# Rotated FFN of a Perceiver block on one NeuronCore: quantised integers turned by transposing DMA transfers, residual added by an accumulating DMA transfer

## The chip, the cores and the metric

The kernel runs on one NeuronCore of a Trainium2 chip. TensorE (PE) multiplies, VectorE (DVE), ScalarE (ACT) and GpSimd (POOL) work on rows of data, SyncE (SP) issues most of the transfers, and 16 DMA engines move the bytes. The metric is the device time of one execution in microseconds (us); lower is better.

## The reference

Three layers follow one another, each on a layer-normalised input and added to its residual: cross attention, a delta-rule attention with an MLP, and a Hadamard-rotated, quantised FFN. Only the last is touched. `x` has 128 x 32 = 4096 tokens of 512 features; the FFN is 2048 wide.

```python
def act_quant(x):
    scale = 127.0 / jnp.clip(jnp.max(jnp.abs(x), axis=-1, keepdims=True), EPS)
    return jnp.clip(jnp.round(x * scale), -128.0, 127.0) / scale

def h_bitlinear(x, w):
    xq = act_quant(fwht(x))      # fwht: normalised Hadamard transform of the last axis
    wq = weight_quant(w)         # -1, 0, 1 times one scale
    return jnp.einsum('bsh,oh->bso', xq, wq)

gate = h_bitlinear(h, w_gate)
up = h_bitlinear(h, w_up)
x = x + h_bitlinear(jax.nn.silu(gate) * up, w_down)    # h = layernorm(x)
```

## The kernel before

The function `hadamard_ffn` works on 32 tiles of 128 tokens. The weights lie in SBUF as bf16 integers (`wg`, `wu`, `wd`); two DRAM arrays come from the stage before: `x2`, the residual, and `z2`, the centred rows after the first butterflies of the first Hadamard transform.

One tile goes through these steps, by the lines of the kernel before:

- `load` (932): SP loads a `zt` tile of `z2` three tiles ahead, and an `xt` tile of `x2` for the residual.
- `turned` (969-970): TensorE transposes `zt` (through the helper at line 97), ScalarE copies it to `zT`. `rotated` (939): four products with the 128 x 128 Hadamard matrix finish the transform in PSUM.
- `integers` (976-981): VectorE takes the row maximum (976) and works out a scale (948, 950, 951); `rounded` multiplies and adds a magic number on ScalarE (956) and subtracts it on VectorE (960) or, where its last argument is true, on ScalarE (958). The result `q` is bf16, 128 x 512.
- `integers_turned` (986): TensorE transposes `q` in four blocks into PSUM, ScalarE copies them to `qT`.
- `middle` (996-1002): in four groups of 512 columns, TensorE multiplies by `wg` and by `wu`; ScalarE applies SiLU (1001), VectorE multiplies both (1002) into `m`, 128 x 2048 in fp32.
- `butterflies` (126, 127): eight VectorE additions and subtractions on halves of `m`.
- `middle_turned` (1008-1009) and `rotated` (939): sixteen fp32 transposes of `m`, four copies to `mT` on ScalarE, sixteen products with the Hadamard matrix into four PSUM banks.
- `last_integers` (1016-1026): four maxima (1016), their maximum (1020), the scale, and four roundings into `q2`; ScalarE subtracts the magic number for groups 0 and 2, VectorE for 1 and 3.
- `last_turned` (1032-1033): sixteen bf16 transposes of `q2` on TensorE in two PSUM tiles, two copies to `q2T` on ScalarE.
- `finish` (1039-1043): sixteen products with `wd`, scaling on ScalarE into `xo` (1041), the residual `xt` added on POOL (1042), and a store that POOL issues (1043).

The loop at the end (1055-1083) lays several tiles over one another: in turn `i` it works on the first integers of tile `i+1`, the middle of tile `i`, the rotation and last integers of tile `i-1` and the finish of tile `i-2`. A scheduler puts the instructions of each engine into a fixed order, and each engine then runs its own list in that order, waiting on semaphores where an operand or a buffer isn't ready. All PSUM tiles of this stage share one pool of eight banks (`ps`), so a product can have to wait until an earlier bank has been read. SP's transfers are issued in order; an SP instruction that waits holds all behind it.

Of the kernel before, what the change touches and what calls it, by code (L numbers as in the profile page):

```python
# [11 lines left out]
BF = mybir.dt.bfloat16  # L12
AF = mybir.ActivationFunctionType
ALU = mybir.AluOpType
# [4 lines left out]
P = 128  # L19
D = 512  # L20
DC = D // P
# [12 lines left out]
IF = 2048  # L34
IC = IF // P
# [83 lines left out]
def butterflies(nc, a, b):  # L119

    n = a.shape[1] // P
    step = 1
    while step < n:
        i = a.rearrange("p (a c d) -> p a c d", c=2, d=step * P)
        o = b.rearrange("p (a c d) -> p a c d", c=2, d=step * P)
        nc.vector.tensor_add(o[:, :, 0, :], i[:, :, 0, :], i[:, :, 1, :])  # L126
        nc.vector.tensor_sub(o[:, :, 1, :], i[:, :, 0, :], i[:, :, 1, :])  # L127
        a, b, step = b, a, 2 * step
    return a
# [255 lines left out]
NG = NT // SG  # L385
# [513 lines left out]
def hadamard_ffn(g: Ctx, x2, z2, mv2, had, ffn, out):  # L899


    tc, nc = g.tc, g.nc
    c1, c2 = 1.0 / math.sqrt(D), 1.0 / math.sqrt(IF)
    NG = IF // D
# [5 lines left out]
    with tc.tile_pool(name="d_w", **right) as wp, tc.tile_pool(name="d_w2", **right) as wp2, stack:  # L910
# [19 lines left out]
        def load(i, src, name):  # L930
            t = xp.tile([P, D], FP, name=name)
            nc.sync.dma_start(t, src[i * P : (i + 1) * P, :])
            return t

        def rotated(xT, c0):

            pr = ps.tile([P, D], FP, name="ps")
            for c in range(DC):
                nc.tensor.matmul(  # L939
                    pr[:, c * P : (c + 1) * P], xT[:, c0 + c, :], hd, start=True, stop=True  # L940
                )
            return pr

        def scales(mx, c):


            m = st.tile([P, 1], FP, name="m")
            nc.vector.tensor_scalar(m, mx, c, Q_EPS, ALU.mult, ALU.max)
            qs = st.tile([P, 1], FP, name="qs")
            nc.vector.reciprocal(qs, m)  # L950
            nc.vector.tensor_scalar(qs, qs, c, 127.0, ALU.mult, ALU.mult)  # L951
            return m, qs

        def rounded(q, pr, qs, scalar=False):
            t = wk.tile([P, D], FP, name="t")
            nc.scalar.activation(t, pr, AF.Identity, bias=magic, scale=qs)  # L956
            if scalar:
                nc.scalar.activation(q, t, AF.Identity, bias=minus)
            else:
                nc.vector.tensor_scalar(q, t, MAGIC, None, ALU.subtract)  # L960

        def statistics(ns):

            nc.scalar.activation(rstd[:, ns], mv2[:, ns, 1], AF.Sqrt, bias=g.ln_eps)
            nc.vector.reciprocal(rstd[:, ns], rstd[:, ns])
            nc.vector.tensor_scalar_mul(rstd[:, ns], rstd[:, ns], c1)

        def turned(i):
            zT = wk1.tile([P, DC, P], FP, name="zT")
            nc.scalar.copy(zT, g.transposed(ps, z.pop(i), g.ident))  # L970
            return zT

        def integers(i, pr):

            mx = st.tile([P, 1], FP, name="mx")
            nc.vector.tensor_reduce(mx, pr, AX.X, ALU.max, apply_absolute_value=True)
            m, qs = scales(mx, rstd[:, i : i + 1])
            q = wk1.tile([P, D], BF, name="q")
            rounded(q, pr, qs)
            f = st.tile([P, 2], FP, name="f")  # L980
            nc.vector.tensor_scalar_mul(f, both, m)
            return q, f

        def integers_turned(q, f):
            qT = wk1.tile([P, DC, P], BF, name="qT")
            nc.scalar.copy(qT, g.transposed(ps, q, g.identb, BF))
            return qT, f

        def middle(qT, f):

            m = mp.tile([P, IF], FP, name="m")
            for k in range(NG):
                ks = slice(k * D, (k + 1) * D)
                pg = ps.tile([P, D], FP, name="ps")
                for dc in range(DC):
                    nc.tensor.matmul(pg, qT[:, dc, :], wg[:, dc, ks], start=dc == 0, stop=dc == DC - 1)  # L996
                pu = ps.tile([P, D], FP, name="ps")
                for dc in range(DC):
                    nc.tensor.matmul(pu, qT[:, dc, :], wu[:, dc, ks], start=dc == 0, stop=dc == DC - 1)  # L999
                s = wk.tile([P, D], FP, name="s")  # L1000
                nc.scalar.activation(s, pg, AF.Silu, scale=f[:, 0:1])
                nc.vector.scalar_tensor_tensor(m[:, ks], pu, f[:, 1:2], s, ALU.mult, ALU.mult)  # L1002
                yield m

        def middle_turned(m):
            mT = mp.tile([P, IC, P], FP, name="mT")
            for k in range(NG):
                pt = g.transposed(ps, m[:, k * D : (k + 1) * D], g.ident)
                nc.scalar.copy(mT[:, k * DC : (k + 1) * DC, :], pt)
            return mT  # L1010

        def last_integers(pr):

            mx = st.tile([P, NG], FP, name="mx4")
            for k in range(NG):
                nc.vector.tensor_reduce(  # L1016
                    mx[:, k : k + 1], pr[k], AX.X, ALU.max, apply_absolute_value=True
                )
            mx1 = st.tile([P, 1], FP, name="mx")
            nc.vector.tensor_reduce(mx1, mx, AX.X, ALU.max)  # L1020
            mm, qs = scales(mx1, c2)
            q = mp1.tile([P, IF], BF, name="q2")
            for k in range(NG):
                rounded(q[:, k * D : (k + 1) * D], pr[k], qs, k % 2 == 0)
            f = st.tile([P, 1], FP, name="fd")
            nc.vector.tensor_mul(f, mm, sd)
            return q, f

        def last_turned(q):
            qT = mp1.tile([P, IC, P], BF, name="q2T")  # L1030
            for k in range(2):
                pt = g.transposed(ps, q[:, k * IF // 2 : (k + 1) * IF // 2], g.identb, BF)
                nc.scalar.copy(qT[:, k * IC // 2 : (k + 1) * IC // 2, :], pt)  # L1033
            return qT

        def finish(i, x, qT, f):
            pd = ps.tile([P, D], FP, name="ps")
            for c in range(IC):
                nc.tensor.matmul(pd, qT[:, c, :], wd[:, c, :], start=c == 0, stop=c == IC - 1)  # L1039
            xo = wk.tile([P, D], FP, name="xo")  # L1040
            nc.scalar.activation(xo, pd, AF.Copy, scale=f)  # L1041
            nc.gpsimd.tensor_add(xo, xo, x)  # L1042
            nc.gpsimd.dma_start(out[i * P : (i + 1) * P, :], xo)

        n = NT // P
# [1 line left out]
        rstd = wp.tile([P, n], FP, name="rstd")  # L1049
        z = {i: load(i, z2, "zt") for i in range(3)}  # L1050
        nc.sync.dma_start(wd.rearrange("p c n -> p (c n)"), ffn[2][0])
        x = {}
        statistics(slice(0, late))
        f, m, q = integers_turned(*integers(0, rotated(turned(0), 0))), {}, {}
        for i in range(n + 2):
            if i + 3 < n:
                z[i + 3] = load(i + 3, z2, "zt")
            if i + 1 < n:
                zT = turned(i + 1)
            if i < n:  # L1060
                x[i] = load(i, x2, "xt")
                steps = middle(*f)
                m[i] = next(steps)
            if i == n // 2:
                statistics(slice(late, n))
            if i + 1 < n:
                f = integers(i + 1, rotated(zT, 0))
            if i < n:
                for _ in steps:
                    pass  # L1070
            if 0 <= i - 1 < n:
                mT = middle_turned(m.pop(i - 1))
            if 0 <= i - 2:
                q2, fd = q.pop(i - 2)
                q2T = last_turned(q2)
            if 0 <= i - 1 < n:
                q[i - 1] = last_integers([rotated(mT, k * DC) for k in range(NG)])
            if i + 1 < n:
                f = integers_turned(*f)
            if 0 <= i - 2:  # L1080
                finish(i - 2, x.pop(i - 2), q2T, fd)
            if i < n:
                m[i] = butterflies(nc, m[i], mp.tile([P, IF], FP, name="mb"))

# [2 lines left out]
def perceiver_block(  # L1087
# [26 lines left out]
    with tc.tile_pool(name="s_l", bufs=1, side="right", reuse_waits="tile") as sp:  # L1114
# [9 lines left out]
        def beside_mlp(b):  # L1124
# [9 lines left out]
            x2, z2, mv2, beside_mlp,  # L1134
        )
    hadamard_ffn(g, x2, z2, mv2, had, list(zip(fq, scales)), out)


# [57 lines left out]
```

## Time and profile before

| what | value |
|---|---|
| median of 3 runs | 3079.94 us (3078.09 to 3083.41) |
| the profiled execution | 3080.81 us, its span 3079.0 us |
| rotated FFN in the span | about 2415 to 3079 us |
| busy in the whole span | PE 95%, DVE 67%, ACT 35%, POOL 23% |

The profile is of one execution. Its groups name a line, an engine, an operation and `out<-in` tiles, then the count, the busy time, the mean of one in ns, and the idle time ahead of it with what ended it. Lines 97, 126, 127, 939, 956 to 960 lie in helpers, so groups are told apart by tile names. PEld is the loading of weights into TensorE, beside the products.

### The profile page before, as it was taken

The numbers are of one execution on the slowest core, as the hardware profiler recorded it, in microseconds if no ns is written. First come the engines' busy times: TensorE is split into PE (matmuls) and PEld (weight loads), VectorE is DVE, ScalarE is ACT, GpSimd is POOL, SyncE is SP. The second block draws the span as 40 slices with busy tenths as digits, with TensorE's granted clock in tenths as the row PEclk, the third lists the DMA queues.
The fourth block names the chain that finished last, engine by engine and source line by source line (L and its number), as shares of the span: only waits on it lengthen the run. The fifth ranks groups of instructions, "written<-read, shape, count | busy, mean of one in ns | idle before, by whom it ended". The sixth has DMA issues, their size and how long they took to land.

```text
span 3079.0 us, 42048 instructions
## 1 busy us (share of the span) xinstructions
PE 2934.2 (95%) x15558; PEld 1683.7 (55%) x15558; DVE 2059.5 (67%) x3432; ACT 1090.1 (35%) x1812; POOL 706.0 (23%) x995
## 2 busy tenths in 40 slices
PE   8999999999999999599999999999999899999997
PEld 3444344443333333367676666667777566666664
DVE  2353434326699797378778787878422599999996
ACT  1111111215656666312221112111111366666665
POOL 1121212112686675321212111011000010000001
PEclk9999999999999999799999999999999999999998
DMA  9797989863554544641423323131411111111110
GB/s 332 265 311 269 307 306 310 274 213 98 166 148 131 173 129 132 198 126 59 128 74 106 97 66 112 48 101 50 139 42 42 55 42 42 42 42 35 39 31 21
DMA packets 258236, 408.09 MB, mean 133 GB/s; under 512 B 68336, under 2 KB 170864, under 8 KB 254576
## 3 DMA queue, kind: packets, MB, share of 16 engines
q1 hardware_dynamic: 223856, 305.21, 31.7%
q0 software_dynamic: 34176, 100.19, 9.5%
q8 instruction: 124, 2.03, 0.3%
q14 instruction: 80, 0.66, 0.1%
HBM read 288.36 MB, written 93.85 MB: 124 GB/s over the span
## 4 chain that ended last, share of the span: by engine, by line
PE 41%; DVE 17%; ACT 5%; issue 3%; DMA 2%; SPq 0%; POOL 0%; DVEq 0%; POOLq 0%; ACTq 0%
PE pm L834 9%; PE pm L823 9%; PE pm L826 9%; PE pp L520 5%; PE ps L797 3%; DVE mb L127 3%; ACT t L956 3%; DVE mb L126 2%; DVE mx L1016 2%; DVE m L126 2%; PE pg L455 2%; PE ps L764 2%; DVE m L1002 1%; DVE m L127 1%; DVE W L442 1%
## 5 line engine op out<-in xcount | busy, mean ns | idle before, releaser
L823 PE MATMUL pm<-hT,wg 128*128 128x256 f32 x1408 | 342.1, 386 | 0.7 <-ACT hT L812 0.7
L826 PE MATMUL pm<-hT,wu 128*128 128x256 f32 x1408 | 333.3, 379 | 0.0
L436 DVE TENSOR_TENSOR pr<-L,W 128x1984 f32<-128x1984 f32 (+30 forms) x248 | 312.1, 1258 | 24.6 <-DMA L<-ld 20.6
L442 DVE TENSOR_TENSOR W<-W,pr 128x1984 f32<-128x1984 f32 (+30 forms) x248 | 309.0, 1246 | 3.2
L834 PE MATMUL pm<-wd,mT 128*128 128x512 f32 x704 | 307.2, 592 | 0.0
L823 PEld LDWEIGHTS pm<-hT,wg 128*128 128x128 f32 x1408 | 262.2, 191 | 57.5 <-issue 16.2
L826 PEld LDWEIGHTS pm<-hT,wu 128*128 128x128 f32 x1408 | 267.2, 190 | 36.2
L834 PEld LDWEIGHTS pm<-wd,mT 128*128 128x128 f32 x704 | 132.6, 190 | 160.8 <-issue 160.7
L828 ACT ACTIVATE sg<-pm 128x256 f32<-128x256 f32 x176 | 67.4, 383 | 350.1 <-PE pm L823 340.1
L829 DVE TENSOR_TENSOR mT<-pm,sg 128x256 f32<-128x256 f32 x176 | 73.8, 419 | 164.1 <-PE pm L826 150.0
L1042 POOL TENSOR_TENSOR xo<-xo,xt 128x512 f32<-128x512 f32 x32 | 42.7, 1336 | 581.6 <-ACT xo L1041 581.6
L996 PE MATMUL ps<-wq,qT 128*128 128x512 bf16 x512 | 133.1, 383 | 28.9 <-DVE m L1002 17.3
L956 ACT ACTIVATE t<-ps,magic,qs 128x512 f32<-128x512 f32 x160 | 117.6, 777 | 96.5 <-DVE qs L951 96.4
L461 POOL TENSOR_TENSOR kk<-kk,cm 128x256 f32<-128x256 f32 x128 | 135.5, 1058 | 2.1
L999 PE MATMUL ps<-wq,qT 128*128 128x512 bf16 x512 | 132.4, 381 | 2.2 <-DVE m L1002 2.2
L458 POOL DMA_DIRECT2D ld<-kk x128 | 92.2, 720 | 147.4 <-ACT kk L457 140.4
L346 PE MATMUL ps<-hT,wq 128*128 128x512 f32 x256 | 118.6, 623 | 7.2 <-ACT hT L339 7.2
L939 PE MATMUL ps<-hd,mT 128*128 128x128 f32 x1024 | 121.5, 277 | 0.0
L455 PE MATMUL pg<-kqm,kq 128*32 128x512 f32 x896 | 118.8, 601 | 2.1 <-DMA kqm<-kq 1.5
L302 PE MATMUL ps<-wo,aoT 128*128 128x512 f32 x256 | 118.8, 608 | 1.5 <-ACT aoT L295 1.5
L520 PE MATMUL pp<-hT,wk 128*128 128x512 f32 x256 | 118.6, 604 | 0.3 <-DVE acc L527 0.3
L1039 PE MATMUL ps<-wq,q2T 128*128 128x512 bf16 x512 | 117.2, 383 | 0.9 <-ACT q2T L1033 0.9
(217 smaller groups left out, 5220.6 us busy)
## 6 DMA issues: line engine op xcount, KB each, us to landing
kall<-in_ctxT_dram SPq DMA_DIRECT2D x32, 2056.0 KB
cx<-in_ctx_dram SPq DMA_DIRECT2D x32, 2048.0 KB
x<-xo POOLq DMA_DIRECT2D x64, 256.0 KB, 3.4
xt<-x SPq DMA_DIRECT2D x64, 256.0 KB
ld<-kk POOLq DMA_DIRECT2D x128, 128.0 KB, 2.5
pd<-kk POOLq DMA_DIRECT2D x128, 128.0 KB, 2.3
L<-ld SPq DMA_DIRECT2D x8, 2048.0 KB
pe<-pd SPq DMA_DIRECT2D x256, 64.0 KB
```

The lines of the kernel that those rows point to most:

```text
L126: nc.vector.tensor_add(o[:, :, 0, :], i[:, :, 0, :], i[:, :, 1, :])
L436: nc.vector.tensor_mul(pr[:, 0:n], bc(L[:, s, :, s + 1 : T].rearrange("p h t -> p t h"), HD), w[:, s].unsqueeze(1).to_broadcast([P, n, H4, ...
L442: nc.vector.tensor_sub(w[:, s + 1 :], w[:, s + 1 :], pr[:, 0:n])
L455: nc.tensor.matmul(pg[js], k[:, js], m[:, :, :, js], start=True, stop=True)
L461: nc.gpsimd.tensor_mul(kk[:, 1], kk[:, 1], cm.unsqueeze(1).to_broadcast([P, HH, T]))
L520: nc.tensor.matmul(pp.rearrange("p b t -> p (b t)"), w[n][:, dc, ec * P : (ec + 1) * P], hT[:, dc, :], start=dc == 0, stop=dc == DC - 1,)
L823: nc.tensor.matmul(pg, wg[:, dc, fs], hT[:, dc, :], start=dc == 0, stop=dc == DC - 1)
L826: nc.tensor.matmul(pu, wu[:, dc, fs], hT[:, dc, :], start=dc == 0, stop=dc == DC - 1)
L834: nc.tensor.matmul(pd, mT[:, fc, i * P : (i + 1) * P], wd[:, fc, :], start=fc == 0, stop=fc == FC - 1,)
L956: nc.scalar.activation(t, pr, AF.Identity, bias=magic, scale=qs)
L996: nc.tensor.matmul(pg, qT[:, dc, :], wg[:, dc, ks], start=dc == 0, stop=dc == DC - 1)
L999: nc.tensor.matmul(pu, qT[:, dc, :], wu[:, dc, ks], start=dc == 0, stop=dc == DC - 1)
```

## The change

The first integers `q` and the last integers `q2` are transposed by one transfer each, from SBUF to SBUF, that SP issues, in place of TensorE transposes and ScalarE copies. All four roundings of `q2` end on ScalarE. The first transfer is issued directly after `q` is rounded, inside the turn; the finish moves one turn later (tile `i-3`, in the middle of the turn, so the loop has one more turn). The residual is no longer loaded into a tile and added on POOL: a transfer issued by POOL adds rows of `x2` to `xo` in SBUF, and SP then stores `xo`.

```diff
         def integers_turned(q, f):
             qT = wk1.tile([P, DC, P], BF, name="qT")
-            nc.scalar.copy(qT, g.transposed(ps, q, g.identb, BF))
+            nc.sync.dma_start_transpose(qT, q)
             return qT, f
...
             for k in range(NG):
-                rounded(q[:, k * D : (k + 1) * D], pr[k], qs, k % 2 == 0)
+                rounded(q[:, k * D : (k + 1) * D], pr[k], qs, True)
...
         def last_turned(q):
             qT = mp1.tile([P, IC, P], BF, name="q2T")
-            for k in range(2):
-                pt = g.transposed(ps, q[:, k * IF // 2 : (k + 1) * IF // 2], g.identb, BF)
-                nc.scalar.copy(qT[:, k * IC // 2 : (k + 1) * IC // 2, :], pt)
+            nc.sync.dma_start_transpose(qT, q)
             return qT
 
-        def finish(i, x, qT, f):
+        def finish(i, qT, f):
...
             nc.scalar.activation(xo, pd, AF.Copy, scale=f)
-            nc.gpsimd.tensor_add(xo, xo, x)
-            nc.gpsimd.dma_start(out[i * P : (i + 1) * P, :], xo)
+            nc.gpsimd.dma_start(xo, x2[i * P : (i + 1) * P, :], accum_op=ALU.add)
+            nc.sync.dma_start(out[i * P : (i + 1) * P, :], xo)
...
-        x = {}
         statistics(slice(0, late))
-        f, m, q = integers_turned(*integers(0, rotated(turned(0), 0))), {}, {}
-        for i in range(n + 2):
+        f, m, q, done = integers_turned(*integers(0, rotated(turned(0), 0))), {}, {}, {}
+        for i in range(n + 3):
...
             if i < n:
-                x[i] = load(i, x2, "xt")
                 steps = middle(*f)
...
             if i + 1 < n:
-                f = integers(i + 1, rotated(zT, 0))
+                f = integers_turned(*integers(i + 1, rotated(zT, 0)))
+            if 0 <= i - 3:
+                finish(i - 3, *done.pop(i - 3))
...
-            if 0 <= i - 2:
-                q2, fd = q.pop(i - 2)
-                q2T = last_turned(q2)
             if 0 <= i - 1 < n:
-                q[i - 1] = last_integers([rotated(mT, k * DC) for k in range(NG)])
-            if i + 1 < n:
-                f = integers_turned(*f)
-            if 0 <= i - 2:
-                finish(i - 2, x.pop(i - 2), q2T, fd)
+                q2, fd = last_integers([rotated(mT, k * DC) for k in range(NG)])
+                done[i - 1] = last_turned(q2), fd
```

In the changed kernel's own numbering the large transfer is line 1031, the products with `wd` 1037, `xo` 1039, the accumulating transfer 1040 and the store 1041; the lines up to 1027 keep their numbers.

## Prediction

> **What bounds the kernel now.** I read the profile from coarse to fine: the windows of the last stage, its groups of instructions, its waits, and the timeline of one token tile. The rotated FFN runs from about 2415 to 3079 us of the span. In its steady part the windows show (columns: busy us and instruction count of PE, PEld, DVE, ACT, POOL, then granted clock, DMA share, GB/s):
>
> ```profile
> 2550.00:2650.00 100.00, 94.62 (x647) 63.40 (x646) 91.89 (x149) 63.06 (x100) 9.30 (x11) 1.00 0.13 41
> 2650.00:2750.00 100.00, 94.63 (x646) 63.32 (x644) 91.88 (x148) 63.08 (x101) 9.15 (x10) 1.00 0.14 44
> ```
>
> Two engines are nearly full and the DMA engines are 13% busy. From 2550 to 2950 us line 1016 runs 80 times, four to a tile: 20 tiles in 400 us, **20.0 us a tile**. The groups of that window that the change touches:
>
> ```profile
> L127 DVE TENSOR_TENSOR mb<-m 128x1024 f32<-128x1024 f32 x41 | 72.2, 1761 | 0.0
> ...
> L1033 ACT COPY q2T<-ps 128x1024 bf16<-128x1024 bf16 x40 | 40.3, 1105 | 0.0
> ...
> L958 ACT ACTIVATE q<-t,minus 128x512 bf16<-128x512 f32 x41 | 29.6, 721 | 0.0
> L97 PE MATMUL ps<-identb,q 128*128 128x128 bf16 x400 | 28.9, 219 | 0.0
> L960 DVE TENSOR_SCALAR q<-t 128x512 bf16<-128x512 f32 x61 | 25.8, 423 | 27.2 <-ACT t L956 26.7
> ...
> L986 ACT COPY qT<-ps 128x512 bf16<-128x512 bf16 x20 | 11.7, 586 | 22.9 <-PE ps L97 22.9
> ```
>
> The waits say that ScalarE waits for the second scale, and TensorE for PSUM banks that late evictions hold:
>
> ```profile
> ACT t L956 <- DVE qs L951: 63.8, 21, 3.8
> ...
> PE ps L996 <- DVE m L1002: 13.8, 8, 1.7
> PE ps L996 <- ACT t L956: 8.3, 13, 0.7
> ```
>
> So besides the full engines there is a ring of dependences. The timeline shows one turn, from the end of one rotation (line 939 from mT, which ended at 2701.82) to the end of the next:
>
> ```profile
> 2706.36 1.32 POOL L1042 TENSOR_TENSOR xo<-xo,xt 128x512 f32<-128x512 f32 x1 [17.19 <-ACT xo L1041]
> ...
> 2706.53 2.23 DVE L127 TENSOR_TENSOR mb<-m 128x1024 f32<-128x1024 f32 x1
> ...
> 2709.95 0.14 DVE L951 TENSOR_SCALAR qs<-qs 128x1 f32<-128x1 f32 x1
> ...
> 2710.12 1.45 ACT L956 ACTIVATE t<-ps,magic,qs 128x512 f32<-128x512 f32 x2 [2.60 <-DVE qs L951]
> ...
> 2714.01 0.79 ACT L956 ACTIVATE t<-ps,magic,qs 128x512 f32<-128x512 f32 x1
> ...
> 2714.67 1.86 ACT L1001 ACTIVATE s<-ps,f 128x512 f32<-128x512 f32 x3
> ...
> 2716.38 2.09 ACT L1009 COPY mT<-ps 128x512 f32<-128x512 f32 x4
> ...
> 2717.39 3.79 PE L939 MATMUL ps<-hd,mT 128*128 128x128 f32 x32
> ```
>
> The segments are 8.3 (maxima and scale on VectorE), 3.9 (roundings), 3.4 (SiLU and first copy) and 3.8 us (rotation): 19.4; neighbouring turns take up to 20.6. One butterfly takes 2.23 us beside POOL's residual addition, the others 1.22.
>
> **What the Trainium skill says.** "SBUF — State Buffer", Who interferes with whom: a VectorE instruction with two SBUF inputs contends with a GpSimd instruction that reads SBUF. The trace agrees: 2.23 against 1.22 us. "DMA: Bandwidth & Descriptors", Latency and other measured facts: a DMA transpose reached 261 GB/s; no run here shows one. Same page, SDMA does more than copy: its unit is a 256-byte tile. "VectorE: DVE Perf Modes", The three transpose paths: one 128x128 bf16 block takes 390 ns on TensorE and 1309 ns by DMA.
>
> **The change, part by part, per tile.**
> TensorE loses 20 transposes of integers. In the timeline their two groups hold the queue 0.99 + 0.42 us. PE's issue sum is now 6.86 (lines 996, 999) + 3.42 (1039) + 3.65 + 0.95 (939) + 2.26 + 0.57 (97, fp32) + 1.41 = 19.1; it becomes 17.7. VectorE loses two roundings (2 x 0.43) and the stretch (1.0): 18.4 to 16.5. ScalarE loses 2 x 1.0 + 0.5 of copies and gains two of line 958 (0.61 each in sequence). Neither is the new bound; the ring is, so I add it up in the instruction order of the changed program.
>
> (a) End of rotation to scale. The four reductions of line 1016 now stand after one butterfly and follow the rotation's groups, the last ending about 0.8 after it; then four unstretched butterflies (4 x 1.2) and small operations: 6.0 with the hand-over instead of 8.3.
> (b) Roundings. ScalarE now runs four t (0.67 each), four q (0.61) and xo (0.58) before the next tile's t: 5.7 instead of 3.9.
> (c) That t, three SiLUs (0.57 each) and the first copy: 3.0 instead of 3.4, as the sixteen transposes no longer stand in between.
> (d) Rotation: 3.8.
> Sum 18.5 us, above PE's 17.7. Gain 1.5 us over some 30 steady tiles: **-45**.
>
> **The new path.** Measure from the first t. The second rounding ends at 5.1, the next tile's at 7.1. SP issues the large transpose (512 KB), then the small one (128 KB). The small one is wanted at 13.0, when TensorE begins the next tile. Lower price: 261 GB/s, that is 2.0 and 0.5 us. Upper working price: packets. The DMA view (packets, MB, share of 16 engines' time) of a window of small packets, 1300 to 1400 us, 870 bytes on average:
>
> ```profile
> q1 hardware_dynamic: 10415, 9.06, 31.8%
> ```
>
> and of this stage (2420 to 3079 us; the last figure is the median from issue to landing):
>
> ```profile
> q1 hardware_dynamic: 8127, 15.45, 8.4%
> ...
> out_dram<-xo POOLq DMA_DIRECT2D x32, 256.0 KB, 3.2
> ```
>
> 31.8% of 16 x 100 us over 10,415 is 49 ns each. The large transpose is 2,048 pieces of 256 bytes, 128 to an engine: 6.3 us; the small one 1.6. For issue and first byte I take 1.3 and for landing 0.8 us, an estimate inside the 3.2 us that the 256 KB store takes from issue to landing. By the low price the small one is issued at 7.3, behind nothing that matters, and lands at L = 7.3 + 1.3 + 0.5 + 0.8, about 10. By the high price it stands behind the large one: L = 5.3 + 1.3 + 6.3 + 1.6 + 0.8 = 15.3. From its landing to the end of that tile's rotation TensorE has 17.2 us of work (its 17.7 less the zt transposes), and 6.0 of (a) stands before t, so two periods are at least L + 23.2. At L = 10 or 13 the ring's 18.5 stands; at 15.3 the period is 19.3; at 16.8 it is today's 20.0. I take a price below 5 us for the large one, since DMA is idle otherwise: 18.5.
>
> The large transpose itself has a whole tile of slack: its product moved one tile later. The accumulating transfer replaces POOL's addition; SP's store waits for it, and behind that store stand the next zt load and the next tile's transposes, not due for 13 us. Priced from the 256 KB store's 3.2 up to the 6.3 us that such a store took in the crowded first 300 us, it is hidden: 13 us cover it, and only beyond them would it delay the transposes. POOL's own wait is only for xo.
>
> **Ends.** Filling: wd's 2 MB stand on SP's queue ahead of the first small transpose, and the first tiles have no other PE work to hide one: estimate +4 (0 to 8). Draining: after the last rotation, rounding on ScalarE alone costs +1.2, the transpose instead of PE and copies (2.5 us in the trace) +1.7, accumulate and then store, against a 1.25 addition and a store, +2.5: about +6 (4 to 10).
> Total -45 + 4 + 6 = -35. The profiled execution took 3080.81 (span 3079.0, 1.8 around it), 0.9 above the median of the runs: 3080 - 35 = **3045**. With a ring between 18.0 and 19.0 and both ends at their bounds, 3028 to 3065.
>
> **Rivals.**
> 1. Packets cost what the window says (49 ns). Period 19.3, gain 0.7 x 30 = 21, ends +11: about 3070. For it: the piece size; against it: the skill's measured rate is three times faster. It blends into no change where the period is 19.65 (L 16.1).
> 2. Slower: the two transposes on SP's one queue become the ring. The place is the wait of the next tile's first product (line 996) for qT; the point is where both together take over some 9 us (L above 16.1). Price: in this stage q1's 8,127 packets took 8.4% of 16 x 659 us, 109 ns each. At that, 14 + 3.5 us: L = 25. The first product then frees the first SiLU, which stands on ScalarE ahead of t, and the period is L + 1.7 = 26.7: 6.7 x 31 + 12 = +220, about 3300. If blocks went one after another at 1309 ns (21 + 5.2 us, L 33.7) it would be 35.4 a tile, 3570. For it: a larger transfer stands ahead of the urgent one, and nothing in this trace transposes by DMA. Against it: that rate would leave 16 engines nearly unused.
> 3. The ring stays at 19.6, because ScalarE's longer row of roundings (b) delays the PSUM banks that TensorE waits for: gain 12, ends +10, 3078. Against it: (a) gains more than (b) loses.
>
> **How the numbers follow.** Forecast 0.60 (3045, own range 3028 to 3065); rival 1 0.11; rival 3 0.06; rival 2 0.23. Range 3028 to 3110: it holds the forecast, rivals 1 and 3 and the mild end of rival 2. 0.2% is 6 us, about what a measurement here tells from no change. Faster: the forecast and 0.08 of rival 1, 0.68. Within 0.2%: the other 0.03 of rival 1 and 0.04 of rival 3, 0.07. Slower: rival 2 and 0.02 of rival 3, 0.25.
>
> **What would show it.** Right: some 18.5 us between groups of line 1016; no 2.2 us butterfly; qT landing before TensorE asks; ScalarE's wait for the scale shorter. Wrong: line 996 waiting for a DMA each tile, SP's queue held in the transposes, or ScalarE's t later than 6 us after the rotation.

## The result, and the profile after

The changed kernel takes 3045.19 us (median of 4 runs, 3042.59 to 3050.57), the kernel before, on the same chip, 3081.68 us (3078.09 to 3083.64). The ratio is 0.9885, 95% interval 0.9868 to 0.9902: 1.2% faster. The profiled execution took 3042.59 us, its span 3040.8.

The first product of the FFN for tile 0 and the last rotation of tile 31 divide the stage into three parts, read from the two timelines:

| part of the span, us | before | after | difference |
|---|---|---|---|
| earlier stages, which the change doesn't touch | 2415.0 | 2410.0 | -5.0 |
| filling: first transpose of `zt` to first product of line 996 | 8.0 | 12.0 | +4.0 |
| middle: from there to the end of the last rotation | 633.3 | 590.4 | -42.9 |
| draining: from there to the end | 22.8 | 28.4 | +5.6 |

The first row is no effect: in the traces of all the kernels below, whose earlier stages are the same, that part ends anywhere from 2403.8 to 2415.0 us. So the middle part, which starts inside the stage, is the better measure of a variant, and it is given below beside each median.

In the steady part (2550 to 2950 us) line 1016 runs 88 times, where it ran 80 times: 22 tiles in 400 us where there were 20. Such a count can be off by most of a tile; the ends of the rotations give 18.25 us a tile after 19.8 (alternating 19.3 and 20.6), and tile times below are taken from them. The windows of the changed kernel (columns as before):

```profile
2550.00:2650.00 100.00, 96.26 (x590) 63.40 (x600) 89.53 (x149) 63.16 (x106) 5.51 (x6) 1.00 0.42 82
2650.00:2750.00 100.00, 96.88 (x576) 61.39 (x586) 91.27 (x149) 61.64 (x103) 4.60 (x5) 1.00 0.38 78
```

TensorE does a tile in 18.2 us and is 97% busy, without the 1.4 us a tile of the transposes; DMA went from 13 to about 40%. The groups of the same 400 us:

```profile
L958 ACT ACTIVATE q<-t,minus 128x512 bf16<-128x512 f32 x88 | 58.5, 718 | 0.0
...
L127 DVE TENSOR_TENSOR mb<-m 128x1024 f32<-128x1024 f32 x44 | 53.5, 1216 | 0.0
```

The mean of that butterfly fell from 1761 to 1216 ns: the stretch beside GpSimd's addition is gone. Four ScalarE roundings a tile stand where two stood. The waits (us in total, times, longest):

```profile
ACT t L956 <- DVE qs L951: 75.7, 22, 3.7
...
PEld L996 <- DMA qT<-q: 5.1, 7, 1.1
```

ScalarE still waits for the second scale in every tile, 3.4 us on average (before, 63.8 us in 21 waits, 3.0). TensorE waits for the small transpose in a third of the tiles, by 0.7. One turn, from the end of a rotation to the end of the next:

```profile
2703.82 0.72 PE L939 MATMUL ps<-hd,mT 128*128 128x128 f32 x5
...
2710.04 0.15 DVE L951 TENSOR_SCALAR qs<-qs 128x1 f32<-128x1 f32 x1
...
2710.22 1.45 ACT L956 ACTIVATE t<-ps,magic,qs 128x512 f32<-128x512 f32 x2 [2.90 <-DVE qs L951]
2711.56 1.33 ACT L958 ACTIVATE q<-t,minus 128x512 bf16<-128x512 f32 x2
...
2715.90 0.79 ACT L956 ACTIVATE t<-ps,magic,qs 128x512 f32<-128x512 f32 x1
...
2718.95 3.84 PE L939 MATMUL ps<-hd,mT 128*128 128x128 f32 x32 [0.23 <-ACT mT L1009]
```

From 2704.54 to 2710.22 are 5.7 us (maxima and scale), to 2715.90 another 5.7 (roundings), to 2718.95 3.1 (SiLU and first copy), to 2722.79 3.8 (rotation): 18.25.

The start and the end pay. The first product of the stage, and the end of it:

```profile
2421.99 1.49 PE L996 MATMUL ps<-wq,qT 128*128 128x512 bf16 x3 [9.12 <-DMA qT<-q]
...
3017.91 1.33 ACT L958 ACTIVATE q<-t,minus 128x512 bf16<-128x512 f32 x2
...
3024.94 6.17 PE L1037 MATMUL ps<-wq,q2T 128*128 128x512 bf16 x16 [9.05 <-DMA q2T<-q]
...
3032.12 0.85 POOL L1040 DMA_DIRECT2D xo<-x  x1 [11.17 <-ACT xo L1039]
3036.14 0.33 SPq L1041 DMA_DIRECT2D out_dram<-xo  x1
```

With nothing else to run, TensorE waits for both transposes. The last rounding ends at 3019.24 and the product begins at 3024.94: by the 512 KB transpose 5.7 us pass, though not by it alone, since the accumulating transfer of the tile before is issued at 3020.11 and runs beside it (see the run pool_add). The last accumulating transfer holds the store back by 4.0 us.

### The profile page after: what moved, and what is told of

It reads as the page before. It is cut to its first block, busy times and chain, and to the rows that moved or that the text cites. A ratio compares the mean times of both kernels' runs of the same rounds, so it can differ in the third digit from the quotient of the medians.

```text
span 3040.8 us, 40815 instructions
## 1 busy us (share of the span) xinstructions
PE 2895.6 (95%) x14856; PEld 1647.0 (54%) x14918; DVE 2010.3 (66%) x3368; ACT 1052.8 (35%) x1780; POOL 664.0 (22%) x963
## 4 chain that ended last, share of the span: by engine, by line
PE 38%; issue 23%; DVE 4%; DMA 2%; POOL 1%; ACT 0%; SPq 0%; POOLq 0%; DVEq 0%; ACTq 0%
PE pm L823 8%; PE pm L826 8%; PE pm L834 8%; PE pp L520 5%; PE ps L797 4%; PE pg L455 2%; PE ps L764 2%; DVE W L442 1%; DVE pr L436 1%; DMA xs<-x 1%; POOL xo L1040 1%; DMA wd<-in_WdownT_dram 1%; PE ps L97 1%; PE pm L455 0%; PE pn L579 0%
## 5 line engine op out<-in xcount | busy, mean ns | idle before, releaser
L1040 POOL DMA_DIRECT2D xo<-x x32 | 29.1, 908 | 589.1 <-ACT xo L1039 589.1
L996 PE MATMUL ps<-wq,qT 128*128 128x512 bf16 x453 | 124.3, 381 | 17.1 <-DMA qT<-q 15.3
L999 PE MATMUL ps<-wq,qT 128*128 128x512 bf16 x511 | 132.2, 381 | 1.5
L939 PEld LDWEIGHTS ps<-hd,mT 128*128 128x128 f32 x1024 | 118.7, 194 | 16.4 <-ACT mT L1009 16.1
```

Of the source, the lines that this page charges most:

```text
L939: nc.tensor.matmul(pr[:, c * P : (c + 1) * P], xT[:, c0 + c, :], hd, start=True, stop=True)
```

## The experiments

The prediction's theory: a ring of dependences sets the tile, before and after; the change shortens it where a butterfly was stretched and by moving the reductions, and gives part back where all roundings are on ScalarE. The main rival: TensorE's work sets the tile, and the transposes taken from it are the gain. Where nothing else is said a variant is made from the kernel before, and the ratio is to that kernel, on the same chip.

**accum_alone.** Only the residual: no `xt` load, no addition on GpSimd.

```diff
-            nc.gpsimd.tensor_add(xo, xo, x)
-            nc.gpsimd.dma_start(out[i * P : (i + 1) * P, :], xo)
+            nc.gpsimd.dma_start(xo, x2[i * P : (i + 1) * P, :], accum_op=ALU.add)
+            nc.sync.dma_start(out[i * P : (i + 1) * P, :], xo)
```

> The kernel before with the accumulating transfer alone: POOL's residual addition and the residual's loads go, SP stores; all transposes stay on TensorE. Theory (the ring sets the tile): the 2.2 us butterfly falls to 1.2, so the tile takes about 19.0 to 19.2 us instead of 20.0, TensorE's own 19.1 being the next floor; over 31 tiles -28 us, and the drain adds 2.5: about 3056. Rival (the stretch was hidden behind TensorE): tile unchanged, drain only, about 3084.

3044.09 us, 0.9886 (0.9865 to 0.9907); middle part 602.7. This part alone gives all that the change gives. The butterflies are at 1.22 us; the window of this kernel:

```profile
2650.00:2750.00 100.00, 98.70 (x676) 66.75 (x675) 91.89 (x155) 65.29 (x104) 5.08 (x6) 1.00 0.17 43
```

TensorE is 98.7% busy at 18.8 us a tile: with the ring 1 us shorter, TensorE with all its transposes is practically full. The theory named the mechanism; its size was 12 us too small.

**small_alone.** Only the 128 KB transpose by transfer, issued directly after `q`.

```diff
-            nc.scalar.copy(qT, g.transposed(ps, q, g.identb, BF))
+            nc.sync.dma_start_transpose(qT, q)
...
-                f = integers(i + 1, rotated(zT, 0))
+                f = integers_turned(*integers(i + 1, rotated(zT, 0)))
```

> The kernel before with the small transpose (q to qT) alone by a transfer; everything else, POOL's addition too, as before. Theory (ring): TensorE's queue loses only 0.42 us that does not lie inside the ring's longest part, so at most 0.3 us a tile, against +3 us of filling: 3070 to 3083. Rival (TensorE's sum sets the tile): 0.42 x 31 = -13 and +3: 3072. Rival (the transfer comes late): line 996 waits for it each tile and the time is above 3090.

3073.37 us, 0.9982 (0.997 to 0.9993); middle part 626.9, 19.6 us a tile. The time lies in the range of the theory and next to the 3072 of the first rival, so this run doesn't tell the two apart; the late transfer, which would have been above 3090, is excluded. The stretch is still there:

```profile
L127 DVE TENSOR_TENSOR mb<-m 128x1024 f32<-128x1024 f32 x41 | 71.2, 1736 | 0.0
```

**large_alone.** Only the 512 KB transpose by transfer, with the finish one turn later as the change has it; GpSimd's addition and the shared rounding stay.

```diff
-            for k in range(2):
-                pt = g.transposed(ps, q[:, k * IF // 2 : (k + 1) * IF // 2], g.identb, BF)
-                nc.scalar.copy(qT[:, k * IC // 2 : (k + 1) * IC // 2, :], pt)
+            nc.sync.dma_start_transpose(qT, q)
...
+            if 0 <= i - 3:
+                finish(i - 3, x.pop(i - 3), *done.pop(i - 3))
...
-            if 0 <= i - 2:
-                finish(i - 2, x.pop(i - 2), q2T, fd)
```

> The kernel before with the large transpose (q2 to q2T) alone by a transfer, and the finish one turn later; small transposes on TensorE, POOL's addition kept, roundings shared as before. Theory (ring): the sixteen transposes leave the stretch between the copies and the rotation, and the finish's place moves POOL's addition away from the butterflies: 18.6 to 19.0 us a tile, -35, drain +3: about 3050. Rival (TensorE's sum): 19.1 less 0.99 = 18.1 plus the old 0.9 of waits, 19.0: -31 and +3, 3054. Rival (a late transfer): it has a whole tile of slack, so only a slower filling or draining would show, and nothing would be above 3082.

3032.34 us, 0.9841 (0.9811 to 0.9871); middle part 585.9. It beats the changed kernel by 13 us although it does less of the change: something that it leaves out must cost time. All butterflies take 1.22 us here too, so their stretch went without the addition being removed, as the expectation had it; only a small VectorE instruction (line 981) takes 0.65 us instead of 0.21. The next run tests what the move alone does.

**move_alone.** Only the order: the finish, and with it GpSimd's addition, one turn later; both transposes stay on TensorE.

```diff
-            if 0 <= i - 2:
-                q2, fd = q.pop(i - 2)
-                q2T = last_turned(q2)
+            if 0 <= i - 2 < n:
+                q2, fd = q.pop(i - 2)
+                done[i - 2] = last_turned(q2), fd
...
+            if 0 <= i - 3:
+                finish(i - 3, x.pop(i - 3), *done.pop(i - 3))
...
-            if 0 <= i - 2:
-                finish(i - 2, x.pop(i - 2), q2T, fd)
```

> The kernel before with only the order changed: finish (and with it GpSimd's addition) one turn later, where the changed kernel has it; both transposes stay on TensorE, the roundings stay shared, and the addition stays on GpSimd. If the stretched butterflies (2.23 us beside the addition) are what cost before, the addition now falls beside instructions that it doesn't stretch: all butterflies 1.22 us, the tile at TensorE's floor of 18.8 us as with the accumulating transfer alone, 31 x 1.2 = 37 less, some 3 back for a longer end: 3046 (3040 to 3052). If instead large_alone was fast because TensorE lost the 16 products of the transpose, the tile stays at 20.0 us and the time is 3075 to 3085.

3053.14 us, 0.9925 (0.99 to 0.9951); middle part 609.6. The timeline of this kernel around one addition, and its window:

```profile
2723.49 1.27 POOL L1042 TENSOR_TENSOR xo<-xo,xt 128x512 f32<-128x512 f32 x1 [16.82 <-ACT xo L1041]
```

```profile
2550.00:2650.00 100.00, 98.36 (x680) 66.06 (x679) 88.83 (x154) 67.39 (x109) 10.97 (x12) 1.00 0.13 40
```

The addition still takes 1.27 us and all butterflies take 1.22: what stretched one of them was that they met. With no instruction taken away, 24 us of the middle part go, and TensorE is again 98% busy. The time is 1 us above the range expected.

**large_twice.** The changed kernel, with each large transpose issued a second time, into a tile that nothing reads, ahead of the small one.

```diff
             nc.sync.dma_start_transpose(qT, q)
+            again = mp1.tile([P, IC, P], BF, name="q2X")
+            nc.sync.dma_start_transpose(again, q)
```

> The changed kernel with every large transpose issued twice, the second into a tile that nothing reads, ahead of the small one on SP's queue. Theory (price of the transposes as in the prediction's second rival): the large one's data takes about 3.5 us (5.7 from the last rounding to its first product in the drain, less 2.1), so the small one lands some 3.5 us later than today's 13.5 us after the first rounding, at 17; the period becomes L/2 + 11.6 = 20.1, +1.9 x 31 and +4 at the ends: about 3107. Rival (the transfers are hidden with room to spare): under +8, below 3053. Rival (much slower, the two queue up and the period is L + 1.7 with a second transpose of 6.3): above 3140.

3058.36 us, 0.9935 (0.9913 to 0.9957); middle part 608.1, 17.6 above the changed kernel, 18.9 us a tile. SP's queue and TensorE's waits in this kernel:

```profile
2702.91 1.86 SPq L1031 DMA_TRANSPOSE q2T<-q  x1
2704.82 5.45 SPq L1033 DMA_TRANSPOSE q2X<-q  x1
2710.37 1.22 SPq L986 DMA_TRANSPOSE qT<-q  x1
```

```profile
PEld L996 <- DMA qT<-q: 39.0, 21, 3.0
PE ps L996 <- DMA qT<-q: 26.4, 15, 2.5
```

Doubled, the transfer does become what TensorE waits for in every tile: the place of the prediction's rivals 1 and 2 is right, and so is the period of rival 1. From the first `t` to the product that takes `qT` the timeline has 15.2 us on average, and (15.2 + 23.2) / 2 = 19.2. The expectation missed by 49 us because it made the small transpose land some 3.5 us later; by the timelines its product begins only some 2 us later than in the changed kernel (13.1 on average). The small transpose is issued 12.2 us after the first `t`, where the changed kernel issues it after 7.2, but its product follows 3.0 us after the issue, where that one's takes about 6. So in the changed kernel part of these 6 us is not its own: it is issued while the large one's packets are still moving.

**half_finish.** The changed kernel with 8 of the 16 products of `finish`.

```diff
-            for c in range(IC):
-                nc.tensor.matmul(pd, qT[:, c, :], wd[:, c, :], start=c == 0, stop=c == IC - 1)
+            for c in range(IC // 2):
+                nc.tensor.matmul(pd, qT[:, c, :], wd[:, c, :], start=c == 0, stop=c == IC // 2 - 1)
```

> The changed kernel with 8 of finish's 16 products a tile: half of the down projection is left out, and the output lacks it. TensorE loses 8 x 0.21 = 1.7 us a tile and no wait of the ring changes. If the ring of maxima, roundings, SiLU and rotation sets the tile, as my prediction held, it stays at 18.2 us, TensorE's busy share falls from 97 to about 88%, and the time is 3043 within 4. If TensorE is what sets the tile after the change (96.9% busy), the tile falls until the next floor, VectorE's 16.4 us of work: to 16.5 to 17.0 us, 31 x 1.2 to 1.7 = 37 to 53 us less, about 2992 to 3008.

3040.88 us, 0.9887 (0.9862 to 0.9912); middle part 585.3, still 88 maxima in 400 us.

```profile
2550.00:2650.00 100.00, 89.56 (x541) 62.49 (x540) 86.40 (x145) 63.16 (x105) 4.23 (x5) 0.95 0.41 82
```

TensorE falls to 90%. The turns of this kernel aren't even: two in three take 17.7 us and one takes 19.3, because there the rotation takes 1.6 us longer:

```profile
2628.11 3.84 PE L939 MATMUL ps<-hd,mT 128*128 128x128 f32 x32 [0.97 <-ACT mT L1009]
2645.78 5.46 PE L939 MATMUL ps<-hd,mT 128*128 128x128 f32 x32 [0.97 <-ACT mT L1009]
```

From 2646.6 to 2650.0 the granted clock is one half, and so it is in each of the long turns. That their mean is again 18.2 is chance. In an undisturbed turn TensorE is busy for 15.9 of 17.7 us: it has lost 1.7 us, and the turn 0.55. The four links of such a turn are 6.3, 5.1, 2.5 and 3.8 us, which sum to 17.7 as they sum to 18.25 in the changed kernel; they differ because `xo` and one SiLU stand ahead of the first `t` here. So the ring sets the turn in both, and TensorE's work doesn't. The next run depends neither on the clock nor on this order.

**shared_rounding.** The changed kernel with VectorE taking the second step of groups 1 and 3, as before.

```diff
-                rounded(q[:, k * D : (k + 1) * D], pr[k], qs, True)
+                rounded(q[:, k * D : (k + 1) * D], pr[k], qs, k % 2 == 0)
```

> The changed kernel with VectorE taking the second step of groups 1 and 3 again, as before. My theory: the all-ScalarE rounding made that link 5.7 us where it had been 3.9; shared, the ring falls by 1.0 to 1.8 us, and TensorE's floor of 17.6 us a tile catches it: 31 x 0.5 = 16 us less, about 3030. Rival: TensorE already sets the tile, or VectorE's two steps (0.36 us each or so) land before the maxima and give it back: 3042 to 3048.

3028.61 us, 0.9839 (0.9817 to 0.9861); middle part 581.7. After the first turns one takes 17.0 to 18.4 us, 17.4 on average, but for three of 20.8 to 23.3 (see large_accum). ScalarE's row of this kernel, and its window:

```profile
2703.66 1.45 ACT L956 ACTIVATE t<-ps,magic,qs 128x512 f32<-128x512 f32 x2 [2.92 <-DVE qs L951]
2705.00 0.72 ACT L958 ACTIVATE q<-t,minus 128x512 bf16<-128x512 f32 x1
2705.61 1.44 ACT L956 ACTIVATE t<-ps,magic,qs 128x512 f32<-128x512 f32 x2
2706.94 0.73 ACT L958 ACTIVATE q<-t,minus 128x512 bf16<-128x512 f32 x1
2707.55 0.69 ACT L1039 ACTIVATE xo<-ps,fd 128x512 f32<-128x512 f32 x1
```

```profile
2550.00:2650.00 100.00, 98.49 (x629) 66.68 (x627) 96.22 (x167) 57.70 (x97) 5.21 (x6) 1.00 0.43 88
```

From the first `t` to `xo` are 3.9 us; in the changed kernel they are 5.1 (2710.22 to 2715.33). ScalarE is 62% busy there, so its work was cheap by the busy time and dear by its place: the two roundings stood in the ring. Taken out, they bring 8.7 us of the middle part, and then TensorE and VectorE are both full, 98 and 96%.

**pool_add.** The changed kernel with the residual loaded and added by GpSimd.

```diff
-            nc.gpsimd.dma_start(xo, x2[i * P : (i + 1) * P, :], accum_op=ALU.add)
-            nc.sync.dma_start(out[i * P : (i + 1) * P, :], xo)
+            nc.gpsimd.tensor_add(xo, xo, x)
+            nc.gpsimd.dma_start(out[i * P : (i + 1) * P, :], xo)
```

> The changed kernel with the residual loaded and added by GpSimd and stored from GpSimd's queue, as before; the transposes by transfer, the rounding and the order stay. Theory: where finish now stands, the addition falls beside VectorE's instructions that read PSUM, which it doesn't stretch; all butterflies stay at 1.22 us and the tile at 18.2; only the end changes, the addition and store (about 2 us) standing for the accumulating transfer (5.8): 3041 (3038 to 3045). Rival: the accumulating transfer is what removes the stretch in the changed kernel, and it comes back: 31 x 1.0 more, about 3075.

3038.26 us, 0.9875 (0.9851 to 0.99); middle part 590.6, the changed kernel's within 0.2. With the finish moved and all roundings on ScalarE, the accumulating transfer brings nothing in the steady part. The reason given was not right, though:

```profile
2716.39 1.26 POOL L1040 TENSOR_TENSOR xo<-xo,xt 128x512 f32<-128x512 f32 x1 [16.12 <-ACT xo L1039]
...
2717.01 0.94 DVE L960 TENSOR_SCALAR q<-t 128x512 bf16<-128x512 f32 x1 [1.18 <-ACT t L956]
```

The addition meets a rounding on VectorE, which takes 0.94 us instead of 0.43, in every tile. That is what the Trainium skill's page "SBUF — State Buffer", Who interferes with whom, leads one to expect: it says that a `tensor_scalar` in a mode with two ports contends with GpSimd although it has one input, and that the later one waits for the whole instruction. The addition ends at 2717.65, 0.64 after the rounding was due; the stretch is 0.51, near it and not equal. In which mode the rounding ran no run shows. The stretch costs nothing here: in none of 22 tiles does TensorE wait for `qT`, where in the changed kernel it does in 7, so without the accumulating transfer the small transpose lands earlier. The large one does too. At the end of this kernel no accumulating transfer runs beside it:

```profile
3018.01 1.33 ACT L958 ACTIVATE q<-t,minus 128x512 bf16<-128x512 f32 x2
...
3023.67 5.00 PE L1037 MATMUL ps<-wq,q2T 128*128 128x512 bf16 x16 [7.68 <-DMA q2T<-q]
```

From the last rounding to the product are 4.3 us (4.3 also in large_alone and shared_pool), where the changed kernel, shared_rounding and large_accum, with the accumulating transfer issued 0.8 us behind it, have 5.5 to 5.7.

**shared_pool.** shared_rounding with pool_add's edit.

> The kernel of shared_rounding with the residual loaded and added by GpSimd again, as in pool_add. Theory: with finish where it now stands, the accumulating transfer brings nothing in the steady part and costs 3 to 4 us at the end: 3025 (3021 to 3028). Rival: with VectorE 96% busy and two roundings more on it, the addition meets a butterfly again and stretches it by 1.0 us a tile: 3040 or more.

3031.03 us, 0.9836 (0.9819 to 0.9852); middle part 579.6. By its ratio it is not to be told from shared_rounding. The time falls between the two expectations. A stretch does return, though not on a butterfly:

```profile
L981 DVE TENSOR_SCALAR f<-both,m 128x2 f32<-128x2 f32 x22 | 16.9, 769 | 0.0
```

This instruction takes 214 ns in shared_rounding; line 960 takes 481 ns on average instead of 422. With three of line 960 that is 0.7 us more of VectorE a tile; VectorE is 97% busy and the turns take 17.9 us instead of 17.4. The middle part is still 2 us below shared_rounding's because no turn is longer than 18.2.

**large_accum.** large_alone with accum_alone's edit: the changed kernel but for the shared rounding and the small transpose, which is on TensorE.

> The changed kernel with the small integers turned on TensorE and the roundings shared (the kernel of large_alone with the accumulating transfer). It differs from shared_rounding in the small transpose alone. If TensorE sets the tile there (98.5% busy at 17.4 us a tile), its four products and their waits come back, 0.5 to 0.8 us a tile, less 3.6 of the fill: 3028.6 + 12 to 21 = 3040 to 3050. Rival, from small_alone, where turning the small integers by transfer brought 6 us of 3080: 3027 to 3035, about as large_alone's 3032 with the accumulating transfer's longer end.

3025.11 us, 0.9814 (0.98 to 0.9829); middle part 579.0. The rival is nearly right (its range ends 2 us above). The turns alternate between 17.6 and 18.1 us, 17.9 on average, where shared_rounding, which differs in the small transpose alone, has 17.4 in most. Its waits, beside those of shared_rounding:

```profile
PEld L996 <- ACT qT L986: 10.8, 23, 0.5
```

```profile
PEld L996 <- DMA qT<-q: 6.6, 7, 2.2
```

By transfer the small transpose spares TensorE 0.4 us a tile, and most turns are shorter by as much. What takes it back are the three long turns, in which TensorE waits 4.8, 2.0 and 3.5 us for the transfer. The first of them:

```profile
2502.05 0.34 SPq L1041 DMA_DIRECT2D out_dram<-xo  x1
2502.49 1.23 SPq L986 DMA_TRANSPOSE qT<-q  x1
2504.99 1.89 PE L996 MATMUL ps<-wq,qT 128*128 128x512 bf16 x4 [4.80 <-DMA qT<-q]
```

In this turn the store stands ahead of the small transpose in SP's queue, and it waits 7.6 us for the accumulating transfer; in the steady turns the transpose stands ahead of the store. The changed kernel has one such turn too, with a wait of 1.7 us. In the other two long turns the transpose was issued ahead of the store and still came late; why stays open. From about the end of each wait the granted clock is one half for 3.4 to 6.8 us, which lengthens the turn further. large_alone, large_accum and shared_pool, which share the roundings too, have no such turn: the first two leave the small transpose on TensorE, the third keeps its stores off SP's queue.

large_accum differs from large_alone in the accumulating transfer alone, and there it brings 6.9 us of the middle part: where VectorE is nearly full, the small stretch of line 981 costs. Which of the two nearly full engines holds these kernels, TensorE at 98% or VectorE at 95%, isn't settled.

**ends.** The changed kernel with its first and last tile done as before, and the last residual added by VectorE as it reads PSUM.

```diff
+            if first:
+                nc.scalar.copy(qT, g.transposed(ps, q, g.identb, BF))
+            else:
+                nc.sync.dma_start_transpose(qT, q)
...
+                rounded(q[:, k * D : (k + 1) * D], pr[k], qs, not last or k % 2 == 0)
...
+            if not last:
+                nc.sync.dma_start_transpose(qT, q)
+                return qT
+            for k in range(2):
+                pt = g.transposed(ps, q[:, k * IF // 2 : (k + 1) * IF // 2], g.identb, BF)
...
+            if i == n - 1:
+                nc.vector.scalar_tensor_tensor(xo, pd, f, xl, ALU.mult, ALU.add)
+                nc.sync.dma_start(out[i * P : (i + 1) * P, :], xo)
+                return
```

> The changed kernel with its two ends put back: the first tile's integers and the last tile's are turned on TensorE, the last tile's rounding is shared, and the last residual is loaded ahead and added by VectorE as it reads PSUM, with a plain store. The steady part is the changed kernel's, 18.2 us a tile. Theory: the fill gives back its 3.6 us; at the end the large transfer (5.7 us) gives way to 16 products and two copies (about 3), the accumulating transfer (5.8 us) goes, the rounding is 1.8 shorter: 8 to 10 less there. In all 3045 - 12 = 3033 (3029 to 3037). Rival: the ends were hidden by other waits, and less than 4 us comes back: over 3040.

3029.97 us, 0.983 (0.9814 to 0.9846). Filling 8.0, middle 590.8, draining 21.6: 4.0 and 6.7 us less, the middle unchanged. So the 10 us that the prediction charged to the ends were there, and none of it was needed. The median fell by more than these 10.7 us (15 below the changed kernel's); of the 12.7 us between the two profiled executions, 2.3 lie in the earlier stages.

**shared_ends.** shared_rounding and ends together.

> The kernel of the run shared_rounding with the two ends put back as in the run ends. If the gains add: 3028.6 less 3.6 of the fill and 6 to 8.5 of the end, 3017 (3014 to 3021), about 28 us below the changed kernel and 61 below the kernel before. Rival: TensorE, at 98.5% busy, has to take the first and the last transposes too and the ends give less than half: 3024 or more.

3020.03 us, 0.9798 (0.9784 to 0.9813); filling 8.0, middle 582.0, draining 21.3. By the three parts the gains of the two variants add, and this is the fastest of all runs: 2.0% below the kernel before, some 25 us below the changed one.

```profile
3011.92 0.75 DVE L1048 SCALAR_TENSOR_TENSOR xo<-ps,fd,xt 128x512 f32<-128x512 f32 x1 [9.60 <-PE ps L1045]
```

The last tile no longer waits for a transposing or an accumulating transfer: its sum is ready 15.8 us after the last rotation (2996.88 to 3012.67), where the changed kernel's last accumulating transfer is only issued after 19.7.

## Why the prediction was right, and where its working was off

Four kernels lead from the kernel before to the changed one, each by one part more, so the middle part can be divided:

| kernel | middle, us | step | what came in |
|---|---|---|---|
| before | 633.3 | | |
| accum_alone | 602.7 | -30.6 | residual by transfer: the stretch goes |
| large_accum | 579.0 | -23.7 | large transpose by transfer, finish one turn later |
| shared_rounding | 581.7 | +2.7 | small transpose by transfer: shorter turns, three long ones |
| the changed kernel | 590.4 | +8.7 | all roundings on ScalarE |

Another order divides it differently: with the finish moved first (move_alone, 23.7 of 633.3) the accumulating transfer is worth nothing in the changed kernel (pool_add) and 6.9 with the roundings shared (large_alone against large_accum).

- **The ring as the bound, before and after.** Right. Before, the stretched butterfly held the tile at 19.8 us; after, half_finish shows that TensorE's work doesn't set it, and shared_rounding that 1.2 us less on ScalarE does shorten it. Two of the signs named for it failed all the same: ScalarE's wait for the scale grew, from 3.0 to 3.4 us, and `qT` landed after TensorE asked in a third of the tiles. But the margin was thin: with the changed kernel's transposes TensorE's floor, at most 17.4 us, is 0.8 below the ring, and accum_alone and shared_rounding both ended with TensorE 98% busy.
- **The four links.** Forecast 6.0, 5.7, 3.0 and 3.8; measured 5.7, 5.7, 3.1 and 3.8. The tile came to 18.25 instead of 18.5, from 19.8 instead of the 20.0 that a count of maxima had given; that the two errors cancel is luck. Over 26 steady turns a turn lost 1.55 us, where the forecast had 1.5. The 31 turns lost 45.3 us, the first rotation came 2.4 later, and so the middle part lost 42.9 for a forecast of 45. The range was mis-added: a ring of 18.0 to 19.0 over 30 tiles with both ends at their bounds gives 3024 to 3068, and the result lies in either.
- **TensorE's sums.** 19.1 and 17.7 were both some 0.3 too high: accum_alone runs at 18.8 with all transposes, most turns of shared_rounding at 17.4 with none. The difference of 1.4 was right.
- **The ends.** +4 and +6 forecast, +4.0 and +5.6 measured, and taken back by the run ends.
- **The large transpose.** The price taken, below 5 us, held. In the last tile of the changed kernel its packets move almost alone from 3020.0 to 3023.0 us:

```profile
q1 hardware_dynamic: 2036, 0.52, 92.7%
```

92.7% of 16 x 3.0 us over 2,036 packets is 22 ns each, where the prediction weighed 49 and 109; 128 of them are 2.8 us. With that, rivals 1 and 2 fall; their place was right, as large_twice shows. The low price, 2.0 us by the 261 GB/s of the Trainium skill ("DMA: Bandwidth & Descriptors", Latency and other measured facts), was too low, but far nearer than the upper 6.3. The small transpose still landed later than that price gives: in the turns where TensorE waited for it, 13.1 to 13.9 us after the first `t`, where the sum with 2.8 and 0.7 has 10.9. It was priced as if it met the large one alone; from 2701.2 to 2705.5 us the accumulating transfer takes 35.5% of the engines beside it, and without that transfer TensorE doesn't wait (pool_add).

- **The accumulating transfer.** It took 5.8 us to landing, inside 3.2 to 6.3. SP's store waited 3.2 us a tile for it, hidden as forecast in the steady turns, but not in an early one, where that store stood ahead of a small transpose and TensorE waited 1.7 us.

```profile
xo<-x POOLq DMA_DIRECT2D x32, 256.0 KB, 5.8
```

- **Rival 3** had the right mechanism: ScalarE's longer row of roundings does cost. It costs 0.8 us in most tiles (17.4 to 18.2), not the 1.1 that would have eaten the gain.
- **What the prediction didn't see.** It took the change as one whole. It didn't ask what each part is worth, and so not that the stretch alone was worth nearly all of the result, that moving the addition, with nothing else changed, brings most of it, and that two of the parts give time back in this company.

## What to carry to other kernels

A stretch of one microsecond in a link of a ring is worth a microsecond a turn, and where two instructions contend, moving one of them past the other brings most of what removing it brings (24 and 31 us here). When several edits come together, price each with the others in place: here two engines and a ring stood within 2 us of each other, so the parts don't add, and an edit that relieves a full engine by loading the ring (the roundings) costs what it seemed to save. A transfer that is hidden in the steady part is bare in the first and the last tile; these two can keep the old way.

## What was not expected of the hardware

- A 512 KB transposing transfer of bf16 within SBUF takes 4.3 us from its producer's end to the product in pool_add, large_alone and shared_pool, and 5.5 to 5.7 where an accumulating transfer is issued 0.8 us behind it; its packets move for 2.8. It holds SP's queue for 1.3 to 3.0 us in the changed kernel, and a second one just behind it in large_twice for 2.5 to 6.0.
- GpSimd's addition of 128 x 512 fp32 stretched a VectorE addition of two SBUF operands from 1.22 to 2.23 us, a rounding with one SBUF operand from 0.43 to 0.94, and an instruction on 128 x 2 from 0.21 to 0.77 on average (shared_pool); in move_alone, where the addition meets none of them, all kept their short times.
- With half of one group of products left out (half_finish), the granted clock fell to one half for 3.4 us in every third turn of the steady part; in the changed kernel it stayed at 1.00 there.
